# Layer 3 of a four-layer convolution and attention kernel: key tiles two tile rows away scored in packed pieces, and no zero products for the accumulators

## The chip, the core and the metric

The kernel runs on one core of a Trainium2 chip. Its time is the device time of that core in microseconds (us), taken as the median of several executions. A separate execution is recorded by the hardware profiler; all rows of the profile come from that one.

## The reference, cut to what matters

The input is x of shape (4, 256, 48, 48). Three convolution layers come first, each added to its input; the change does not touch them. Layer 3 is a linear attention over windows, again added to its input:

```python
def _L3_conv_ref(x, Wq, Wk, Wv, Wout, bout):      # x: group-normalised
    HEADS, WINDOWS = 8, (1, 2, 4)
    q = sigmoid(einsum('bchw,oc->bohw', x, Wq))   # 8 heads of 32 channels
    k = sigmoid(einsum('bchw,oc->bohw', x, Wk))
    v = einsum('bchw,oc->bohw', x, Wv); v = v / max(norm(v over a head), 1e-12)
    Ik, Ikv = integral(k), integral(k outer v)    # sums over rows and columns
    for w in WINDOWS:                             # box of 48/w by 48/w around each pixel
        wk, wkv = box(Ik, 48 // w), box(Ikv, 48 // w)
        attn = (q . wkv) / (q . wk + 1e-6)
    return Wout @ concat(attn of the three windows) + bout
```

For every query pixel and each of the three windows (48, 24 and 12 pixels wide) the output is the sum of (q . k) v over the keys inside the window, divided by the sum of q . k.

## The kernel before

**Tiles.** The kernel does not build the integral images of k outer v. It multiplies queries with keys block by block. The image is cut into six tile rows of `RB = 8` pixel rows. A query block is one tile row of one batch and of one half of the channels (4 heads), 384 pixels: `order` holds 4 batches x 2 channel halves x 6 tile rows = 48 blocks. The keys of a tile row `a` are three tiles (`c` = 0, 1, 2) of 8 x 16 = 128 keys each. The half windows are `HALVES = [24, 12, 6]`, so the widest window of a query row `rb` reaches keys with |a - rb| up to 3, the middle window up to 2, and the narrow one up to 1.

**Steps.** A step is one tile row of keys and one half of the query columns (`PARTS[half]`), which is two pieces of 320 and 192 columns (280 and 168 at a distance of 3). `scores` writes q . k for 4 heads into two PSUM tiles `s` (two heads each; the pool `ps_s` has two buffers, so a step takes both). Each piece is one product for each head; the four heads sit on four row groups of TensorE and run beside each other. Then follow four *penalty* products (`picks`, `masks`): in those columns that the widest window sees only in part (`strips`), unseen keys get -1024. `masked` takes the scores out of PSUM into a tile `sm`: `widest` is a Relu over the strips on ScalarE, `middle` multiplies by the mask of the middle window on VectorE, and GpSimd multiplies the middle's result by the mask of the narrow window. `sums` then multiplies `sm` by the values `vs` and adds it up in three PSUM accumulators `acc0..2`, one for each window. Columns that the widest window sees whole need no scores: `whole` adds them from a summed state, once a block.

In `masked` the two engines take turns: ScalarE takes the second PSUM tile while VectorE works on the first, then they swap:

```python
if full:
    widest(act, *second); middle(*first)
    widest(act, *first);  middle(*second)
```

A tile row two away (|a - rb| = 2) has two steps like the near ones, but the middle window sees only 3 or 4 of its 8 pixel rows and the narrow one none. A tile row three away is seen by the widest window alone (both `widest`, one on each engine).

**Order.** Every engine runs its instructions in the order of the program (`InOrder`). In `stream` the steps of all blocks follow one another, near and far alternating (`tiles_of`); step n is scored and masked, then step n - 2 (`LAG = 2`) is summed. Between steps `advance` lets other jobs put in work by cost estimates: projections of the next batch (`proj_ps`), key states (`keys_ps`, `kv_ps`), window sums of k on GpSimd (`k_sums`), `norms` (the denominators: DMA loads, differences and products `nhi` on GpSimd, then `norm_ps` on TensorE), `prepare` and `finish` (division and the output product `out_ps`). `turn` and `bank` let a job go on when the step has TensorE time to spare (`time = 1200 + mask_time - sums_time`), `pool_turn` when it has GpSimd time to spare (3600 ns a step less the narrow masks), and `FETCH` holds a job for three steps after a load. `until` makes a step wait, in program order, until a job has been issued: at the start of block i everything for `("done", i - 2)`, in whatever order the jobs then come.

**Accumulators.** `begin` opens a block. `acc1` and `acc2` are first written whole by a product of zeros (`tiled(acc, zeros[:, 0:P], zeros, start=True, stop=False)`), so that every later product can add.

Of the kernel before, what the change touches and what calls it, by code (L numbers as in the profile page):

```python
# [140 lines left out]


# [3 lines left out]
def penalties():  # L146

    got = []
    for half in range(2):
        got.append(((0, half), strips(half), None))  # L150
    for da, (r0, r1) in FAR_ROWS.items():
        for half in range(2):
            got.append(((da, half), PARTS[half], (r0, r1)))
    return got
# [93 lines left out]
def conv_preact_kernel(  # L248
# [1374 lines left out]
    with (  # L1623
# [24 lines left out]
        zeros = wts.tile([P, NB], BF16, name="zeros")  # L1648
        nc.gpsimd.memset(zeros, 0.0)
# [258 lines left out]

        class Block:


            def __init__(self, i, qs):
                self.i, self.qs = i, qs
                self.b, self.ct, self.rb = b, ct, rb = order[i]
                self.tiles = tiles_of(rb)
                self.todo = [
                    [(a, half) for a, half in self.tiles if seen(wi, a, rb)] for wi in range(NW)
                ]
                self.accs = self.stage = None

            def scores(self, a, half):
                r0, r1 = rows_seen(0, a, self.rb)
                ss = [ps_s.tile([P, 2, 512], F32, tag="s", name="s") for _ in range(NPR)]
                at = 0
                for c, x0, x1 in PARTS[half]:
                    n = (x1 - x0) * (r1 - r0)
                    for pr, s in enumerate(ss):
                        for j in range(2):
                            head = slice((2 * pr + j) * D, (2 * pr + j + 1) * D)
                            pe.matmul(  # L1930
                                s[:, j, at : at + n],
                                kvs[self.b, self.ct, a][0][head, c, :],
                                self.qs[head, x0:x1, r0:r1],
                                start=(at == 0),
                                stop=False,
                            )
                    at += n
                lo, hi = strip_columns(half) if rows_whole(a, self.rb) else (0, at)
                first, n = PENALTY_AT[(0 if rows_whole(a, self.rb) else a - self.rb), half]
                for pr, s in enumerate(ss):  # L1940
                    for j in range(2):
                        g = 2 * pr + j
                        rows = slice(g * D, g * D + RB + KC)
                        pe.matmul(
                            s[:, j, lo:hi],
                            picks[rows, :],
                            masks[rows, PEN_AT + first : PEN_AT + first + n],
                            start=False,
                            stop=True,
                        )  # L1950
                return ss

            def parts(self, wi, a, half):

                if wi == 0:
                    return strips(half) if rows_whole(a, self.rb) else PARTS[half]
                return parts_seen(wi, half)

            def masked(self, a, half, ss):

                rb = self.rb
                r0, r1 = rows_seen(0, a, rb)
                wis = [wi for wi in range(NW) if seen(wi, a, rb)]
                full = rows_whole(a, rb)
                offset = {PARTS[half][0][0]: 0}
                offset[PARTS[half][1][0]] = (PARTS[half][0][2] - PARTS[half][0][1]) * (r1 - r0)
                left = {c: x0 for c, x0, _ in PARTS[half]}

                t = smp.tile([P, NPR * SM_ROOM], F32, tag="sm", name="sm")
                at, blocks_, views = 0, [], {}  # L1970
                for wi in wis:
                    y0, y1 = rows_seen(wi, a, rb)
                    ps = self.parts(wi, a, half)
                    for c, p0, p1 in ps:
                        if wi == 0:
                            continue
                        n = HG * (y1 - y0) * (p1 - p0)
                        views[wi, c] = t[:, at : at + n].rearrange(
                            "p (j x r) -> p j x r", j=HG, r=y1 - y0
                        )  # L1980
                        at += n
                    if wi > 0:
                        continue
                    n = sum(p1 - p0 for _, p0, p1 in ps) * (y1 - y0)
                    block = t[:, at : at + HG * n].rearrange("p (j n) -> p j n", j=HG)
                    blocks_ = [block[:, 2 * pr : 2 * pr + 2] for pr in range(NPR)]
                    at, o = at + HG * n, 0
                    for c, p0, p1 in ps:
                        m = (p1 - p0) * (y1 - y0)
                        views[wi, c] = block[:, :, o : o + m].rearrange(  # L1990
                            "p j (x r) -> p j x r", r=y1 - y0
                        )
                        o += m
                assert at <= NPR * SM_ROOM

                def times_mask(engine, wi, c, rows, cols, dst, src):
                    mr = rb * RB + rows[0] - (a * RB - HALVES[wi] + 1)
                    mc = cols[0] - (c * KC - MCOL0[wi])
                    nr, ncol = rows[1] - rows[0], cols[1] - cols[0]
# [5 lines left out]
                many = seen(NW - 1, a, rb)  # L2005

                def middle(s, pr):
                    y0, y1 = rows_seen(1, a, rb)
                    for c, p0, p1 in parts_seen(1, half):
                        at = offset[c] + (p0 - left[c]) * RB  # L2010
                        src = s[:, :, at : at + (p1 - p0) * RB].rearrange(
                            "p j (x r) -> p j x r", r=RB
                        )[:, :, :, y0:y1]
                        dst = views[1, c][:, 2 * pr : 2 * pr + 2]
                        times_mask(dve, 1, c, (y0, y1), (p0, p1), dst, src)

                def widest(engine, s, pr):
                    dst = blocks_[pr]
                    n = dst.shape[2]
                    lo, hi = strip_columns(half) if full else (0, n)  # L2020
                    if engine is act:
                        act.activation(dst, s[:, :, lo:hi], AF.Relu)
                    else:
                        dve.tensor_scalar_max(dst, s[:, :, lo:hi], 0.0)

                first, second = zip(ss, range(NPR))
                if full:
# [7 lines left out]
                if many:  # L2035
                    (y0, y1), (z0, _) = rows_seen(2, a, rb), rows_seen(1, a, rb)
                    seen1 = {c: p0 for c, p0, _ in parts_seen(1, half)}
                    for c, p0, p1 in parts_seen(2, half):
                        src = views[1, c][:, :, p0 - seen1[c] : p1 - seen1[c], y0 - z0 : y1 - z0]
                        times_mask(pool, 2, c, (y0, y1), (p0, p1), views[2, c], src)  # L2040
                return views

            def begin(self):
# [4 lines left out]
                for acc in self.accs[1:]:  # L2048
                    tiled(acc, zeros[:, 0:P], zeros, start=True, stop=False)
# [16 lines left out]
            def sums(self, wi, a, half, sms):  # L2066

                todo, acc = self.todo[wi], self.accs[wi]
                r0, r1 = rows_seen(wi, a, self.rb)
                for k, (c, p0, p1) in enumerate(self.parts(wi, a, half)):  # L2070
                    for j in range(HG):
                        pe.matmul(
                            acc[D * j : D * (j + 1)].rearrange("p (w r) -> p w r", w=W)[
                                :, p0:p1, r0:r1
                            ],
                            kvs[self.b, self.ct, a][1][:, c, j, :],
                            sms[wi, c][:, j],
                            start=(wi == 0 and (a, half) == todo[0] and k == 0),
                            stop=((a, half) == todo[-1] and k == 1),
                        )  # L2080
                if (a, half) == todo[-1]:
# [5 lines left out]

        def seen(wi, a, rb):
# [3 lines left out]
        def tiles_of(rb):  # L2092


            tiles = [
                (a, half)
                for a in sorted(range(NRB), key=lambda a: abs(a - rb))
                for half in range(2)
                if seen(0, a, rb)
            ]  # L2100
            near = [t for t in tiles if seen(NW - 1, t[0], rb)]
            far = [t for t in tiles if t not in near]
            both = min(len(near), len(far))
            return [t for pair in zip(near, far) for t in pair] + near[both:] + far[both:]
# [106 lines left out]
        for a in dict.fromkeys(a for a, _ in tiles_of(0)):  # L2211
# [39 lines left out]
        def done(i):  # L2251
# [11 lines left out]
            (i, a, c, n, n == len(tiles_of(rb)) - 1)  # L2263
            for i, (b, ct, rb) in enumerate(order)
            for n, (a, c) in enumerate(tiles_of(rb))
# [116 lines left out]
```

## Time and profile before

| | us |
|---|---|
| median of 3 executions | 3206.32 (3204.66 to 3215.53) |
| profiled execution, device time | 3220.09 |
| its span, first to last instruction | 3218.3 |
| its first score product (layer 3) | 1412.0 |
| TensorE busy in the span | 2886.4 |
| VectorE, ScalarE, GpSimd busy | 2004.0, 1018.9, 1351.2 |

The profile shows for each engine when it was busy; PE is TensorE's products, PEld its weight loads (they overlap), DVE is VectorE, ACT ScalarE, POOL GpSimd, SP the queue that issues most DMAs. Every instruction of the kernel has one line number, that of the helper which issues it, so that groups are told apart by the names of their tiles: `s<-qs,ks` are scores, `s<-masks` penalties, `sm<-s` and `sm<-s,masks` the masking, `acc<-sm,vs` the sums. One score or sum product of the program appears as two records[...].

### The profile page before, as it was taken

The page shows a single profiled execution, that of the slowest core. Times are in us where ns is not written, and L with a number is a line of the kernel's source. Part 1 is how long each engine was busy: PE and PEld are TensorE (multiplying, and loading weights), DVE is VectorE, ACT ScalarE, POOL GpSimd, SP SyncE. Part 2 cuts the span into 40 slices and gives each one's busy share as a digit, 9 for nine tenths or more (in the row PEclk, how much of TensorE's full clock was granted, in tenths as well). Part 3 has the DMA queues.
Part 4 walks back from the last instruction along what each step waited for, and adds up shares of the span by engine and source line. Part 5 has one row for each costly group of instructions (what it writes and reads, how often), then busy time and mean ns, then how long its engine had stood idle before and what let it go on. Part 6 is the DMA issues. An engine that isn't in the chain of part 4 may idle for free.

```text
span 3218.3 us, 97296 instructions
## 1 busy us (share of the span) xinstructions
PE 2886.4 (90%) x41802; PEld 2014.6 (63%) x41802; DVE 2004.0 (62%) x3907; ACT 1018.9 (32%) x2090; POOL 1351.2 (42%) x1916
## 2 busy tenths in 40 slices
PE   3678999899989978889996999998999999999999
PEld 2456768678776857576663665565566665666665
DVE  7976668647855731466774765676546775455454
ACT  0002211111111153326642335552336533333322
POOL 0000021003001221146788776877846777634443
PEclk9789899999999997989998999999999999999999
DMA  8746513431342253224466555554734455501222
GB/s 273 213 158 196 162 53 116 130 107 60 125 132 92 74 152 114 103 89 140 157 207 173 172 167 164 167 171 152 193 91 145 141 173 162 160 33 54 86 68 67
DMA packets 380033, 433.85 MB, mean 135 GB/s; under 512 B 129844, under 2 KB 335444, under 8 KB 378452
## 3 DMA queue, kind: packets, MB, share of 16 engines
q1 hardware_dynamic: 378403, 425.76, 42.9%
q8 instruction: 331, 5.42, 0.7%
q0 software_dynamic: 144, 1.08, 0.2%
q10 hardware_dynamic: 1056, 0.79, 0.1%
q14 instruction: 99, 0.80, 0.1%
HBM read 287.91 MB, written 140.68 MB: 133 GB/s over the span
## 4 chain that ended last, share of the span: by engine, by line
PE 60%; DVE 12%; POOL 4%; DMA 4%; ACT 4%; issue 3%; SPq 2%; ACTq 0%; DVEq 0%; POOLq 0%
PE s L244 16%; PE cv L244 15%; PE acc L244 14%; PE out_ps L244 5%; PE proj_ps L244 5%; DVE sm L244 3%; PE ap L244 2%; ACT sm L244 2%; SPq L244 2%; DVE l2v L244 2%; POOL nhi L244 1%; POOL sm L244 1%; DVE v L244 1%; PE keys_ps L244 1%; DVE x L244 1%
## 5 line engine op out<-in xcount | busy, mean ns | idle before, releaser
L244 DVE TENSOR_TENSOR sm<-s,masks 128x448 f32<-128x448 f32 (+11 forms) x1536 | 634.6, 470 | 465.5 <-PE s L244 431.5
L244 POOL TENSOR_TENSOR sm<-sm,masks 128x704 f32<-128x704 f32 (+11 forms) x512 | 595.2, 1184 | 559.1 <-DVE sm L244 558.7
L244 ACT ACTIVATE sm<-s 128x384 f32<-128x384 f32 (+2 forms) x864 | 467.5, 545 | 783.1 <-PE s L244 641.0
L244 PE MATMUL s<-qs,ks 32*128 32x320 f32 (+3 forms) x7680 | 601.6, 402 | 46.7 <-ACT sm L244 41.6
L244 PE MATMUL cv<-vx,wt 128*128 128x288 f32 x2080 | 561.6, 426 | 91.1 <-DVE vx L244 49.6
L244 PE MATMUL acc<-sm,vs 128*32 128x128 f32 (+20 forms) x17920 | 607.4, 279 | 1.4 <-issue 1.4
L244 PEld LDWEIGHTS s<-qs,ks 32*128 32x128 f32 x7680 | 376.9, 186 | 278.1 <-issue 111.0
L244 PEld LDWEIGHTS acc<-sm,vs 128*32 128x32 f32 x17920 | 430.2, 110 | 190.5 <-issue 137.6
L244 PEld LDWEIGHTS cv<-vx,wt 128*128 128x128 f32 x2080 | 403.4, 198 | 213.0 <-issue 54.1
L244 POOL MEMSET v<- 128x16 f32 (+1 forms) x120 | 18.7, 216 | 761.1 <-DVE vx L244 634.3
L244 PE MATMUL cv<-v,wl 128*128 128x384 f32 x1152 | 227.9, 358 | 25.1 <-issue 8.0
L244 PEld LDWEIGHTS cv<-v,wl 128*128 128x128 f32 x1152 | 217.7, 198 | 36.6 <-issue 16.4
L244 DVE TENSOR_SCALAR sm<-s 128x896 f32<-128x896 f32 (+1 forms) x96 | 110.9, 1155 | 144.4 <-PE s L244 125.4
L244 PE MATMUL s<-masks 24*128 24x192 bf16 (+2 forms) x1920 | 175.5, 268 | 0.0
L244 POOL TENSOR_TENSOR v<-l2v,v 128x384 fp32r<-128x384 f32 x96 | 108.5, 1160 | 119.3 <-ACT v L244 110.6
L244 PE MATMUL cv<-pad,wl 128*128 128x384 bf16 x864 | 145.5, 331 | 5.1 <-ACT pad L244 5.1
L244 POOL TENSOR_TENSOR nhi<-nhi,nq 128x384 f32<-128x384 f32 x144 | 147.8, 1048 | 0.0
L244 PEld LDWEIGHTS <-wl 128*128 128x128 bf16 x864 | 84.5, 98 | 65.6 <-issue 8.1
L244 PE MATMUL out_ps<-o,wout_sb 128*32 128x384 f32 x1152 | 119.8, 487 | 4.9 <-DVE res L244 2.2
L244 DVE TENSOR_TENSOR pt<-cs 128x184 f32<-128x184 f32 x144 | 119.8, 836 | 0.1
L244 PE MATMUL out_ps<-stage,wout_sb 128*32 128x384 f32 x1152 | 119.4, 486 | 0.0
L244 PE MATMUL ap<-seen,xT 120*128 120x120 f32 (+3 forms) x832 | 118.8, 302 | 0.0
(178 smaller groups left out, 3434.7 us busy)
## 6 DMA issues: line engine op xcount, KB each, us to landing
wt<-wt SPq DMA_DIRECT2D x48, 768.0 KB
kb_d<-pt SPq DMA_DIRECT2D x48, 576.0 KB
rc<-r_d SPq DMA_DIRECT2D x192, 144.0 KB
nhi<-kb_d SPq DMA_DIRECT2D x120, 192.0 KB
nlo<-kb_d SPq DMA_DIRECT2D x88, 192.0 KB
o_d<-stage SPq DMA_DIRECT2D x24, 576.0 KB
o<-o_d SPq DMA_DIRECT2D x24, 576.0 KB
wl<-wl_d SPq DMA_DIRECT2D x16, 768.0 KB
```

What stands on the lines that cost most here:

```text
L244: return lambda *args, **kwargs: self.tc.keep_in_program_order(op(*args, **kwargs))
```

## The change

- The steps are objects (`Step`, `steps_of`) that list their pieces. Near tile rows and those three away keep their two steps each.
- A tile row two away gets one step for both halves that scores only the strips: three pieces of 128 columns (two strips of 64 in one for the middle key tile), 384 columns, and one set of penalties of 384 columns.
- For the middle window of such a tile row only the 3 or 4 pixel rows that it sees are scored, in three pieces (84, 117 and 81 columns for 3 rows; 112, 156 and 108 for 4). They are packed, the largest first, into the strip steps up to 512 columns, and what does not fit goes into a further step that has no strips, no penalties and no Relu. A block with one such tile row has two steps for it as before, a block with two has three in place of four.
- The order within a block becomes: two near steps, then packed or far and near steps alternating, then the rest.
- No zero products: `alike` cuts a sum's piece where some of its columns have been written and some not, and a product to new columns overwrites.
- The penalty table has 384 more columns; `zeros` is not made.

The core of the diff:

```diff
+            def add_strips(self, a):
+                begin = self.columns
+                for c, ranges in STRIPS.items():
+                    at = self.add(a, c, ranges, (0, RB))
+                    self.parts[0].append((a, c, ranges, (0, RB), at, self.columns - at))
+                self.penalties.append((begin, self.columns, PENALTY_AT[0, "strips"][0]))
+                self.lo, self.hi = begin, self.columns
...
+            def add_middle(self, a, c):
+                p0, p1 = cols_seen(1, c)
+                rows = rows_seen(1, a, self.rb)
+                at = self.add(a, c, [(p0, p1)], rows)
+                self.parts[1].append((a, c, [(p0, p1)], rows, at, self.columns - at))
...
+        def steps_of(rb):
...
+                elif abs(a - rb) < FAR:
+                    packed.append(Step(rb))
+                    packed[-1].add_strips(a)
...
+            for n, a, c in sorted(middles, key=lambda m: -m[0]):
+                fits = [st for st in packed if st.columns + n <= 512]
+                if not fits:
+                    packed.append(Step(rb))
+                    packed[-1].lo = packed[-1].hi = 0
+                    fits = packed[-1:]
+                fits[0].add_middle(a, c)
+            far = packed + far
+            got, near = near[:2], near[2:]
+            both = min(len(near), len(far))
+            got += [t for pair in zip(far, near) for t in pair]
+            return got + near[both:] + far[both:]
...
-            def scores(self, a, half):
+            def scores(self, st):
...
-                for c, x0, x1 in PARTS[half]:
-                    n = (x1 - x0) * (r1 - r0)
+                for a, c, ranges, (r0, r1), at, n in st.products:
...
-                                self.qs[head, x0:x1, r0:r1],
+                                of_columns(self.qs[head], ranges, r0, r1),
...
                 first, second = zip(ss, range(NPR))
-                if full:
+                if st.parts[1]:
                     widest(act, *second)
                     middle(*first)
                     widest(act, *first)
...
-                for acc in self.accs[1:]:
-                    tiled(acc, zeros[:, 0:P], zeros, start=True, stop=False)
+                self.reached = [set() for _ in range(NW)]
...
+            def alike(self, wi, ranges, nr):
+                new = [x not in self.reached[wi] for x0, x1 in ranges for x in range(x0, x1)]
+                if all(new) or not any(new):
+                    return [(ranges, 0, len(new) * nr)]
+                ((x0, x1),) = ranges
+                cuts = [0, *(n for n in range(1, len(new)) if new[n] != new[n - 1]), len(new)]
...
-                            start=(wi == 0 and (a, half) == todo[0] and k == 0),
+                                start=not self.reached[wi],
```

## Prediction

> **What bounds the kernel now.** I read the page first, then the chain of waits by stretch, the timeline of TensorE inside a step, the groups by shape, and last the waits where the chain leaves TensorE.
>
> ```profile
> span 3218.3 us, 97296 instructions
> ...
> PE 2886.4 (90%) x41802; PEld 2014.6 (63%) x41802; DVE 2004.0 (62%) x3907; ACT 1018.9 (32%) x2090; POOL 1351.2 (42%) x1916
> ...
> PE 60%; DVE 12%; POOL 4%; DMA 4%; ACT 4%; issue 3%; SPq 2%; ACTq 0%; DVEq 0%; POOLq 0%
> ```
>
> TensorE is busiest and holds most of the chain that ended last. Layer 3 runs from 1412 to 3218 us; the change lies there alone. By batch and channel half (the starts of the blocks lie at 1432, 1657, 1918, 2148, 2388, 2601, 2822 and 3009 us) the chain's TensorE share differs, here for the weakest stretch and the strongest:
>
> ```profile
> by line: PE s L244 18.4%; PE acc L244 16.7%; PE out_ps L244 9.8%; POOL nhi L244 9.4%; SPq L244 7.5%; DMA rc<-r_d 5.6%; POOL sm L244 4.7%; issue 3.6%; DVE sm L244 3.3%; DMA n_d<-ns 2.5%; DMA o<-o_d 2.5%; DMA nhi<-kb_d 2.0%; PE keys_ps L244 1
> ...
> by line: PE acc L244 33.0%; PE s L244 31.6%; PE proj_ps L244 21.4%; PE out_ps L244 3.7%; DMA o<-o_d 2.9%; DVE sm L244 2.9%; SPq L244 2.8%; PE keys_ps L244 1.2%; DVE pt L244 1.1%; ACT sm L244 1.0%; issue 0.6%; DVE ss L244 0.3%; PE kv_ps L244
> ```
>
> The first is batch 1's second half (2148 to 2388): TensorE 46%, and the norms' work (nhi, its DMAs and their issue) much of the rest. The second is batch 2's first half: TensorE 91%. The same view gives 84, 49, 65, 46, 91, 74, 76 and 86% for the eight halves in order.
>
> The rates come from the starts of successive groups on TensorE:
>
> ```profile
> 2399.56 0.83 PE L244 MATMUL out_ps<-stage,wout_sb 128*32 128x384 f32 x8
> 2400.32 1.15 PE L244 MATMUL s<-qs,ks 32*128 32x320 f32 x16
> 2401.29 0.26 PE L244 MATMUL s<-masks 24*128 24x192 bf16 x4
> 2401.48 0.96 PE L244 MATMUL acc<-sm,vs 128*32 128x168 f32 x16
> 2402.26 0.83 PE L244 MATMUL out_ps<-o,wout_sb 128*32 128x384 f32 x8
> 2402.91 0.83 PE L244 MATMUL out_ps<-stage,wout_sb 128*32 128x384 f32 x8
> ...
> 2407.43 0.51 PE L244 MATMUL acc<-zeros 128*32 128x384 bf16 x8
> 2407.75 0.56 PE L244 MATMUL acc<-sm,vs 128*32 128x224 f32 x8
> ```
>
> Four heads' products of 384 columns take 0.65 us (2402.26 to 2402.91), 1.68 ns a column; a step's 512 score columns take 0.97, that is 0.86 at this rate and 0.1 once for the first weight load; 192-column penalties 0.19; a block's zeros 0.32. TensorE is thus paid by columns, and idle time in the chain matters as much as the sums.
>
> ```profile
> 2908.72 0.86 PE L244 MATMUL acc<-sm,vs 128*32 128x112 f32 x32
> 2908.77 0.43 SPq L244 DMA_DIRECT2D vs<-v_d  x1
> 2908.82 1.22 DVE L244 TENSOR_TENSOR sm<-s,masks 128x160 f32<-128x160 f32 x4 [1.40 <-PE s L244]
> 2908.91 1.06 ACT L244 ACTIVATE sm<-s 128x384 f32<-128x384 f32 x2 [1.87 <-PE s L244]
> 2909.51 0.38 POOL L244 TENSOR_TENSOR kv<-state 128x96 f32<-128x96 f32 x1
> 2909.97 0.85 POOL L244 TENSOR_TENSOR kv<-kv,state 128x96 f32<-128x96 f32 x2
> 2910.02 0.97 PEld L244 LDWEIGHTS s<-qs,ks 32*128 32x128 f32 x15 [0.60 <-ACT sm L244]
> ```
>
> This is a step two rows away in batch 3, where little else fills TensorE: scores 1.16, masking 1.2, then TensorE waits for ScalarE before it scores again. Such a step's loop is 2.6 us there, against 3.2 to 3.35 in batches 0 to 2, where filler products hold it.
>
> **The change part by part.** There are 64 pairs of block and tile row two away, half with 3 seen rows and half with 4: 128 steps become 112 (14 for 16 in each half of a batch). TensorE work, by the rates above:
>
> - Score columns: 1024 a pair become 384 + 282 (3 rows) or 384 + 376 (4 rows). Saved 358 and 264 columns, 0.60 and 0.44 us; times 32 each: 33.4 us.
> - Penalties: 128 sets of 192 at 0.19 become 64 of 384. Between 192 (0.19) and the 448-column set (starts 2418.66 to 2418.95 on the same timeline, 0.29) a set of 384 is 0.27. 24.3 - 17.1 = 7.2 us saved.
> - Step heads: 16 fewer steps, each about 0.1 us of exposed load at its head and 0.1 before the sums: 3.4 us.
> - Zeros: 48 x 0.32 = 15.4 us.
> - Sums: the same columns; some pieces are cut to 16 (48 groups) and 32 columns (96 groups).
>
> For those cuts a row stands against a rule. The nearest row:
>
> ```profile
> 2915.41 0.37 PE L244 MATMUL kv_ps<-vs,keys 128*32 128x32 f32 x24
> ```
>
> 24 records in 0.37 us, of which about 0.19 is the tail of the last: some 8 ns from one to the next, 60 ns for eight. The Trainium skill (TensorEngine Tiling (Array Packing), Instruction Overhead) says that each product costs about 60 cycles however few columns it has, which is 25 ns, or 200 ns for eight. By the rule the 144 small groups cost 144 x 0.2 = 29 us, by the row 144 x 0.06 = 8.6; their columns alone are 6.4. I take the row: 2.2 us lost (rule: 22). On the score side no row is near: the trace's smallest score piece has 168 columns, 84-column pieces none. The skill (TensorE: Matmul & The Clock Gate, LDWEIGHTS (loading the stationary operand)) prices a load by its columns over 1.2 GHz, 107 ns for 128 columns, and the 0.1 us at a step's head agrees. A pass over 81 to 117 columns streams for 68 to 98 ns, less than the load. Ends: nothing (loads hidden, as for every piece shown) and, as an estimate from that page, 2 x 107 ns a piece in place of 1.68 a column: 168 ns for each pair with 3 rows and 59 for each with 4, times 32 = 7.3 us. I take the 7.3.
>
> Sum: 33.4 + 7.2 + 3.4 + 15.4 - 2.2 - 7.3 = 50 us of TensorE work, 6.25 in each of the eight halves.
>
> What of it is on the path: the chain's TensorE share. Batches 0 to 2: 6.25 x (0.84 + 0.49 + 0.65 + 0.46 + 0.91 + 0.74) = 25.6 us. In batch 3 the loop of scores and masking counts. ScalarE: 384 elements 492 ns, 896 elements 918 ns, so 768 about 812; VectorE: 120 elements 282 ns, 224 elements 390, 320 elements 485, so 234 about 400 and 312 about 475. A strip step masks in 2 x 0.81 = 1.62 (ScalarE; the turns on a PSUM tile leave VectorE's 0.40 beside it), loop 1.22 + 0.2 + 1.65 = 3.1. The further step has VectorE alone: 1.3, 1.7 or (both rows, four pieces) 3.0 us after 0.5, 0.55 or 0.9 of scores, loops 2.0, 2.45, 4.1. One row away twice: 3.1 + 2.0 or 2.45 against 2 x 2.6; two rows: 6.2 + 4.1 against 10.5. Nothing is gained there. I count 2.5 us for each half of batch 3, from the stretches where output products fill TensorE. Together 30.6 us.
>
> Against it: the four-piece step (16 of them) holds TensorE 4.1 us, while its own scores, a near step's sums (848 columns, 1.42) and one filler of 1.3 make 3.6: up to 0.5 x 16 = 8 us if all bind, less where GpSimd or norms bind anyway. And the waits move, as the next part says. I take 5 us for both. VectorE and ScalarE lose 20 us of work each, off the path. The longer mask table is one GpSimd-queue DMA (1051 KB, landed in 8.6 us at 1146) long before its use: nothing, under 1 us if its cover were gone. SP issues as many DMAs as before. The memset dropped (0.41 us at 1394) is nothing.
>
> Net: 25 us off the profiled execution (3220 to 3195). That one stands 14 us above the median; off the median: 3181.
>
> **The rivals.** *A. All of it pays (3156, 22%).* The fillers flow, the loads hide: the whole 50 us. For: batches 0 to 2 are mostly paid by columns. Against: half shares of 46 and 49%.
>
> *B. Swallowed (3199, 17%).* The late norms set the end of batches 0 and 1, and what TensorE saves before a forced wait is waited there.
>
> ```profile
> 1722.38 3.40 PE L244 MATMUL norm_ps<-nhi,head_sel 128*32 128x384 f32 x6 [15.64 <-POOL nhi L244]
> 1727.99 3.15 PE L244 MATMUL norm_ps<-nhi,head_sel 128*32 128x384 f32 x6 [2.22 <-POOL nhi L244]
> ```
>
> This is such a wait: at a block's start everything open is issued at once and TensorE stands for GpSimd (twelve nhi operations of about 1 us a norm and the loads). That block lasts 65 us where its like lasts 36. The gain is then that of batches 2 and 3 alone (15.3 us) less the four-piece steps in full (8): 7 us.
>
> *C. Slower (3222, 9%).* The plan gives GpSimd 3.6 us a step; 16 steps fewer are 58 us fewer for norms and window sums, whose work is the same. In the fixed instruction order of the two programs, four whole norms sit in one bunch at a block's start before, five after, one of them new in batch 2's second half; the first bunch after the change holds two. A bunch costs 20 (56 against 36 us in batch 1) to 30 us. Against: the outputs of the first block of batch 0's second half leave their bunch and are spread over steps. If two bunches are added and none leaves, 2 x 23 - 31 = +15 us; it decides from the second on.
>
> *D. The change doesn't do what it says (2%).* The instruction order shows the dropped zeros and pieces, so hardly.
>
> **How the numbers follow.** My forecast (25 us off) has 50%: 3181, own range 3166 to 3196. Range over the cases: 3148 (A with a lighter bunch) to 3208 (B whole and the light end of C); about a fifth is left out. A measurement tells about 0.3%, 10 us, from no change: faster is below 3196.7. Forecast, A and a third of B make 0.77; the rest of B and D 0.14; C 0.09.
>
> **What would show it.** Right: score columns down by 8% (19,900 of 242,700), no zeros rows, GpSimd busy the same, steps two rows away at 3.1 and 2 to 4 us in batch 3, first halves of batches 0 to 2 shorter by 4 to 6 us each. Loads: 84-column score pieces spaced by 0.21 us for four heads (hidden: 0.14). Wrong: norm_ps waits on nhi (42.9 us on weight loads now) grown by 20 us or more, or sums of 16 columns spaced by 0.2 us.

## The result and the profile after

| | before | after |
|---|---|---|
| median of 6 executions, us | 3209.27 (3204.66 to 3216.24) | 3193.94 (3186.31 to 3198.54) |
| ratio of after to before, 95% interval | | 0.9948 (0.9928 to 0.9967) |
| profiled execution, us | 3220.09 | 3194.66 |
| layer 3 in the profile, first score product to the last instruction, us | 1806.3 | 1781.1 |

The change makes the kernel faster by 0.5%: 15 us in the medians (11 to 23 by the interval), 25 us between the two profiled executions. The single executions of one kernel differ by up to 37 us in this study (one execution of before is left out: it took 4086 us, with TensorE granted 0.65 of its full clock). Part of it lies ahead of the change: in the profiles layer 3 begins anywhere from 1390 to 1416 us. So beside each ratio I also give the length of layer 3 in the profile. Such a length is that of one execution, and no better than that: the profile of before stands 11 us above the median of its kernel, so of the 25 us between the profiles not all is the change.

The page of the changed kernel, with the lines that answer to those shown of before:

```profile
span 3192.8 us, 98649 instructions
...
PE 2866.5 (90%) x42698; PEld 2024.3 (63%) x42698; DVE 2002.8 (63%) x3779; ACT 994.5 (31%) x1965; POOL 1356.8 (42%) x1915
...
PE 62%; DVE 11%; POOL 4%; DMA 4%; ACT 3%; issue 2%; SPq 2%; ACTq 0%; DVEq 0%; POOLq 0%
...
L251 PE MATMUL s<-qs,ks 32*128 32x320 f32 (+10 forms) x8704 | 589.1, 360 | 34.7 <-ACT sm L251 20.1
L251 PE MATMUL acc<-sm,vs 128*32 128x128 f32 (+19 forms) x18432 | 606.0, 276 | 6.3 <-issue 6.2
...
L251 PE MATMUL s<-masks 24*128 24x192 bf16 (+3 forms) x1664 | 168.3, 284 | 0.0
```

The dropped work shows: score products have more records but 222,800 columns in place of 242,700 (records by columns, over the groups by shape), there is no group with zeros, and GpSimd is as busy as before. The span is 25 us shorter, and TensorE keeps its 90%.

The chain of waits, first for batch 1's second half (2122 to 2350 us), then for batch 2's first (2350 to 2568) and second half (2568 to 2799):

```profile
by line: PE s L251 30.9%; PE acc L251 25.8%; PE out_ps L251 16.5%; DVE sm L251 4.2%; POOL nhi L251 3.6%; ACT sm L251 2.7%; PE norm_ps L251 2.6%; PE proj_ps L251 2.6%; issue 2.3%; PE keys_ps L251 1.9%; DMA nlo<-kb_d 1.7%; PE kv_ps L251 0.6%;
...
by line: PE acc L251 31.7%; PE s L251 28.5%; PE proj_ps L251 18.1%; SPq L251 3.9%; PE out_ps L251 3.6%; DVE sm L251 3.4%; DMA v_d<-vt 2.5%; PE keys_ps L251 1.5%; issue 1.5%; DVE pt L251 1.2%; POOL sm L251 0.9%; DVE cs L251 0.7%; PE kv_ps L2
...
by line: PE s L251 20.0%; PE acc L251 18.7%; PE out_ps L251 13.8%; POOL sm L251 7.4%; POOL nhi L251 6.4%; DMA nq<-qr_d 4.9%; DMA res<-x_d 3.8%; SPq L251 3.8%; PE norm_ps L251 3.4%; issue 3.1%; DVE sm L251 2.1%; DMA rc<-r_d 2.1%; ACT sm L251
```

TensorE's share went from 46 to 81% in the first, from 91 to some 83% in the second, and from 74 to 56% in the third. (These windows, like those of the prediction, begin some 11 us after the halves do. Cut at the halves, 2137, 2377, 2590 and 2811 us before and 2111, 2339, 2557 and 2788 after, the shares are 41, 96 and 68% before and 82, 87 and 51% after.) The share of a stretch is thus no property of the stretch that a change leaves alone: the norms (nhi, their DMAs and what waits for them) left one half and came up in another. By half (from one half's last copy of an accumulator to the next one's), in us:

| batch, half | 0,1 | 0,2 | 1,1 | 1,2 | 2,1 | 2,2 | 3,1 | 3,2 |
|---|---|---|---|---|---|---|---|---|
| before | 232.7 | 252.5 | 238.7 | 235.6 | 218.1 | 211.6 | 196.4 | 206.2 |
| after | 223.8 | 244.6 | 231.0 | 228.3 | 218.0 | 230.7 | 188.6 | 200.1 |

Six halves gain 6 to 9 us each, one nothing, and batch 2's second half loses 19.

That loss is one bunch at the start of a block, TensorE alone:

```profile
2620.26 0.85 PE L251 MATMUL norm_ps<-nhi,head_sel 128*32 128x384 f32 x6
2624.57 3.70 PE L251 MATMUL norm_ps<-nhi,head_sel 128*32 128x384 f32 x6 [3.46 <-POOL nhi L251]
2628.83 0.85 PE L251 MATMUL out_ps<-o,wout_sb 128*32 128x384 f32 x8 [0.56 <-ACT ns L251]
...
2636.90 0.83 PE L251 MATMUL out_ps<-stage,wout_sb 128*32 128x384 f32 x8
2637.54 1.65 PE L251 MATMUL acc<-sm,vs 128*32 128x224 f32 x56
```

Everything that the block must have is issued at once: a norm's products, which wait for GpSimd, and twelve groups of output products one after the other until 2637.54. The step around it lasts 20.6 us, from 2618.5. Two things can be lost: the waiting, some 7.6 us from 2621 on, and the outputs as fillers, which then lack beside the masking of the later steps. The second is argued; no run shows it.

### The profile page after: what moved, and what is told of

It is laid out like the page before. It is cut to its first block, busy times and chain, and to the rows that moved or that the text cites. A ratio compares the mean times of both kernels' runs of the same rounds, so it can differ in the third digit from the quotient of the medians.

```text
span 3192.8 us, 98649 instructions
## 1 busy us (share of the span) xinstructions
PE 2866.5 (90%) x42698; PEld 2024.3 (63%) x42698; DVE 2002.8 (63%) x3779; ACT 994.5 (31%) x1965; POOL 1356.8 (42%) x1915
## 4 chain that ended last, share of the span: by engine, by line
PE 62%; DVE 11%; POOL 4%; DMA 4%; ACT 3%; issue 2%; SPq 2%; ACTq 0%; DVEq 0%; POOLq 0%
PE s L251 16%; PE cv L251 15%; PE acc L251 15%; PE out_ps L251 5%; PE proj_ps L251 5%; PE ap L251 3%; DVE sm L251 2%; DVE l2v L251 2%; SPq L251 2%; POOL sm L251 2%; POOL nhi L251 1%; ACT sm L251 1%; DVE v L251 1%; PE keys_ps L251 1%; DVE x L251 1%
## 5 line engine op out<-in xcount | busy, mean ns | idle before, releaser
L251 DVE TENSOR_TENSOR sm<-s,masks 128x448 f32<-128x448 f32 (+9 forms) x1408 | 619.9, 497 | 437.1 <-PE s L251 379.5
L251 ACT ACTIVATE sm<-s 128x384 f32<-128x384 f32 (+2 forms) x736 | 441.5, 609 | 746.6 <-PE s L251 589.7
L251 PE MATMUL s<-qs,ks 32*128 32x320 f32 (+10 forms) x8704 | 589.1, 360 | 34.7 <-ACT sm L251 20.1
L251 PE MATMUL acc<-sm,vs 128*32 128x128 f32 (+19 forms) x18432 | 606.0, 276 | 6.3 <-issue 6.2
L251 PEld LDWEIGHTS acc<-sm,vs 128*32 128x32 f32 x18432 | 443.0, 110 | 190.2 <-issue 143.4
L251 PEld LDWEIGHTS s<-qs,ks 32*128 32x128 f32 x8704 | 395.1, 186 | 256.2 <-issue 112.0
L251 PE MATMUL s<-masks 24*128 24x192 bf16 (+3 forms) x1664 | 168.3, 284 | 0.0
```

The source lines that it names most:

```text
L251: return lambda *args, **kwargs: self.tc.keep_in_program_order(op(*args, **kwargs))
```

## The experiments

Three explanations stood against each other. *The masking and the columns*: the change brings what its columns bring, and the order of the norms takes part of it back. *Conservation*: waits for norms that are taken out of one block come up in another, so the mending of one bunch brings nothing. *Little by itself*: with the norms gone the change would bring only about 20 us, since TensorE is not what a step two rows away waits for. In the expectations Theory 2 is the first of these, Theory 1 the prediction's reckoning, by the chain's TensorE share and with a plan that hardly matters, and Theory 3 that the masking sets the length of a step. "Profile" below is layer 3 in one profiled execution.

**No zeros, alone and left out.** The first kernel is before without its zero products (`begin` keeps a set of written columns and `sums` cuts at it), the second is after with them:

```diff
 # before, begin()
-for acc in self.accs[1:]:
-    tiled(acc, zeros[:, 0:P], zeros, start=True, stop=False)
+self.reached = [set() for _ in range(NW)]
 # after, begin()
-self.reached = [set() for _ in range(NW)]
+self.reached = [set(), set(range(W)), set(range(W))]
+for acc in self.accs[1:]:
+    tiled(acc, zeros[:, 0:P], zeros, start=True, stop=False)
```

> The kernel before without its zero products (a product to columns not yet written overwrites); pieces, steps and every planner decision as before. Theory 1 (TensorE columns pay by the chain's TensorE share, about 0.7): 15.4 us of products less, 11 us off, ratio to before 0.9965. Rival (a block starts while TensorE waits for the masking anyway): 0 to 3 us, ratio 0.999 to 1.000.

> The changed kernel with the zero products put back; its steps, packing and planner decisions unchanged. The difference to the changed kernel (ratio 0.9948) is the worth of the zeros in the new order. Theory 1: 11 us slower than the changed kernel, ratio to before 0.998. Rival (zeros hidden): as the changed kernel, 0.995.

Measured: 0.9988 (0.9969 to 1.0007), profile 1797.0 (before 1806.3), and 0.9943 (0.9920 to 0.9965), profile 1782.4 (after 1781.1). So by the ratios the zeros are worth some 4 us in the one (9 between the profiles), which the interval doesn't tell from nothing, and nothing in the other. Both are nearer to the rival than to 11 us. In the step that holds them the saving is there (of the steps up to 5.5 us the mean is 3.51 without and 3.70 with them in the first pair, 3.80 and 4.04 in the second), but over a block it is not kept.

**The plan's price of GpSimd.** After with another number for the GpSimd time of a step, and nothing else:

```diff
-pool_time = 3600.0 - far_time(stream[n][1])
+pool_time = 3800.0 - far_time(stream[n][1])   # second kernel: 3724.0
```

> The changed kernel with 3800 ns of GpSimd time planned for a step in place of 3600; the same products. In the fixed order this removes the new bunch of norms in batch 2's second half (and the one in the middle of batch 1's second half). Theory 2 (the change saves about 45 us and bunches that come of fewer steps give 20 to 30 back): batch 2's second half falls from 231 to about 211 us, and the time by 20 us against the changed kernel, ratio to before about 0.988. Theory 1 (the plan hardly matters): ratio as the changed kernel's, 0.995, within 0.003.

> The changed kernel with 3724 ns of GpSimd time planned for a step (the loss of 16 steps in 480 made good). In the fixed order the bunch of batch 2's second half stays, and one appears at the start of batch 1's second half. Theory 2: batch 2's second half stays near 230 us, and the time is that of the changed kernel or 5 to 10 us above, ratio 0.995 to 0.998. If it is the size of the allowance as such and not the bunches that counts: as with 3800, ratio 0.988.

Measured: 0.9969 (0.9954 to 0.9984), profile 1790.6, and 1.0026 (1.0012 to 1.0040), profile 1811.2. With 3800 the bunch in batch 2's second half is gone (218.1 us, from 230.7), and batch 1's second half is better too (216.4, from 228.3). But batch 1's first half went from 231.0 to 246.1, batch 2's first from 218.0 to 225.3. With 3724, 250.5 and 237.8 in batch 1. The same instructions in a slightly different order are 25 us apart (3219.09 against 3193.94), more than the change itself brings. Theory 2 missed both times: the bunch went with 3800, and the 20 us did not come, while with 3724 the kernel is slower than either expectation had it.

**Without the norms' differences and products on GpSimd.** Before and after, both without these two operations:

```diff
-pool.tensor_sub(hi[:, wi, n:RB], hi[:, wi, n:RB], lo[:, wi, n:RB])
-pool.tensor_mul(flat, flat, qf)
```

> The kernel before without the differences and products of the norms on GpSimd (about 240 us of GpSimd work; the denominators are then not those of the reference). Loads, planner and all other instructions as before. Theory 2 (what a bunch at a block's start waits for is the norms' GpSimd work): the excess of steps over 5.5 us, 129 us in the profile of before, falls to about 70 and the time by about 50 us, ratio to before 0.984. Theory 1 (GpSimd is off the path): 0 to 10 us, 0.997 or more.

> The changed kernel without the differences and products of the norms on GpSimd (the denominators are then not those of the reference); planner and all other instructions as in the changed kernel. Theory 2 (the change is worth 45 us where no bunch takes it back): ratio to before 0.970, 45 us below e5. If the change is worth 15 to 25 us wherever it stands: 15 to 25 us below e5, ratio 0.977 to 0.979 if e5 comes to 0.984.

Measured: 0.9901 (0.9871 to 0.9930) and 0.9827 (0.9799 to 0.9854); 22 us between the two medians, 13 in the profiles (1763.6 and 1750.3). Both kernels gain less than Theory 2 had named, and the difference is the 15 to 25 us of the other expectation.

**The norms held back.** After, where a norm of a later block may not put its products on TensorE while a block's start issues what it must have:

```diff
 # norms(), ahead of the products
+while hold and (b, rb) > hold[-1]:
+    yield 1
 # at the start of block i
+hold.append((order[i - 2][0], order[i - 2][2]))
 until(("done", i - 2))
+hold.pop()
```

> The changed kernel; while a block's start forces the outputs of the block two before, the norms of later tile rows are held back and come in the steps after. The same work. In the fixed order three of the five whole norms leave the bunches. Theory 2: batch 0's and batch 2's second halves lose about 15 us each, 20 us or more in all against the changed kernel, ratio to before 0.988. Rival (conservation: norms held back here are waited for in a later bunch, as e3's were): ratio 0.994 to 0.997, with the stalled steps elsewhere.

Measured: 0.9949 (0.9933 to 0.9966), profile 1780.2: as after. The waits of weight loads on nhi, 46.7 us in after, are gone from the list of waits, and no time came of it: batch 1 has 238.2 and 234.2 (from 231.0 and 228.3), batch 0's second half 231.3 (from 244.6), batch 2's second half 224.5. In batch 1 the wait came back under another name, an output product that waits for its factor from the same GpSimd:

```profile
2188.22 1.51 PE L251 MATMUL out_ps<-o,wout_sb 128*32 128x384 f32 x8 [13.65 <-POOL o L251]
2189.50 1.50 PE L251 MATMUL out_ps<-stage,wout_sb 128*32 128x384 f32 x8
```

There the wait is conserved.

**The middle's pieces not packed.** After with a further step of its own for the middle of every tile row two away, as many score columns as after but 480 steps, as before:

```diff
-fits = [st for st in packed if st.columns + n <= 512]
-if not fits:
-    packed.append(Step(rb))
-...
-fits[0].add_middle(a, c)
+if a not in own:
+    own[a] = Step(rb)
+    own[a].lo = own[a].hi = 0
+own[a].add_middle(a, c)
+packed = [t for pair in zip(packed, own.values()) for t in pair]
```

> The changed kernel without sharing: each tile row two away has a strip step of 384 columns and a middle step of its own with three pieces; the same score columns, 480 steps as before the change. Columns alone: 16 step heads more (3.4 us), ratio 0.996. Theory 3 (the masking loop counts: 2.9 us for a strip step and 2.8 for a middle step, 5.7 for a tile row against about 5.2 packed, where masking binds): 10 us slower than the changed kernel, 0.998. Theory 2: with 480 steps the bunch of batch 2's second half is not there, 10 us less: 0.992 to 0.995.

Measured: 1.0050 (1.0032 to 1.0067), profile 1824.6. All the expectations missed: with the columns saved and the zeros gone it is slower than before. Part of it is again a bunch, at the start of batch 3, where nothing had stood before:

```profile
2806.86 3.39 PE L251 MATMUL norm_ps<-nhi,head_sel 128*32 128x384 f32 x6 [3.05 <-POOL nhi L251]
2813.64 3.39 PE L251 MATMUL norm_ps<-nhi,head_sel 128*32 128x384 f32 x6 [3.39 <-POOL nhi L251]
```

The rest of the explanation comes from counting, after the next pairs.

**A block may finish one block later.** Before and after with a third `stage` tile and the demand of a block's start put off by one block; two `kvp` buffers are given up for the room:

```diff
-tc.tile_pool(name="kvp", bufs=2 * NRB, reuse_waits="tile")
+tc.tile_pool(name="kvp", bufs=2 * NRB - 2, reuse_waits="tile")
-self.stage = op.tile([P, NW, NB], F32, tag="stage", name="stage")
+self.stage = op.tile([P, NW, NB], F32, tag="stage", name="stage", bufs=3)
-if i >= 2:
-    until(("done", i - 2))
+if i >= 3:
+    until(("done", i - 3))
```

> The kernel before with three stage tiles in place of two, so that a block's start forces the outputs of the block three before, not two (the key pool gives up two of twelve buffers for the room). The same work. In the fixed order whole norms in bunches fall from four to two. Theory 2 (late norms forced at a block's start cost 10 to 25 us each): ratio to before 0.990 to 0.994. Conservation (what isn't waited for here is waited for later): 0.998 or more.

> The changed kernel with three stage tiles in the same way. Whole norms in bunches fall from five to two, and the one of batch 2's second half is gone. Theory 2: that half falls from 231 to about 208 us, ratio to before about 0.984, and against e9 the change is worth 25 to 35 us. Conservation: ratio 0.993 to 0.996.

Measured: 0.9963 (0.9951 to 0.9975) and 0.9848 (0.9824 to 0.9872; 3160.94 us), profiles 1784.8 and 1756.8. The second is faster than both kernels of this case: 33 us below after. Between the two medians the change is worth 35 us here (3196.31 and 3160.94), 28 in the profiles; the profile of the first stands 19 us below the median of its kernel. The first ratio lies between the two expectations, the second is where Theory 2 had it: here conservation does not hold. The weight loads' waits, first before with the third tile, then after with it:

```profile
PEld s L244 <- ACT sm L244: 94.1, 167, 3.0
...
PEld norm_ps L244 <- POOL nhi L244: 17.5, 19, 3.9
```

```profile
PEld s L251 <- ACT sm L251: 71.2, 118, 2.8
...
PEld norm_ps L251 <- POOL nhi L251: 21.4, 14, 4.9
```

The columns are us in total, times, and the longest. The waits for nhi were 42.9 and 46.7 with two tiles; the wait for the masking is what the change itself lowers. Batch 2's second half is at 206.7 us, batch 2's first at 243.4: one long step remains there (29.7 us at 2290).

**No norms at all.** Before and after with the denominators set to one: no loads, no GpSimd work and no products for them, only the inverse and what follows.

```diff
-loaded = [load(ct) for ct in range(NCT)]
-... (differences, products, norm_ps, ns)
+pool.memset(nr, 1.0)
 start(inverse(b, rb, nr, ...))
```

> The kernel before without the norms: no loads, GpSimd work, products or stores for the denominators; ones are written in their place by the same last step, so that everything after it stands. Takes away what the bunches wait for, in the plan and on the chip. Theory 2: ratio to before 0.975 to 0.98.

> The changed kernel without the norms in the same way. The difference to e11 is the worth of the change where no norm is late. If the change pays by TensorE's columns and only the norms take it back (Theory 2): 40 us below e11, ratio to before 0.963 to 0.967. If its worth is about 20 us by itself, as e5 against e6 has it: 20 us below e11, 0.969 to 0.974.

Measured: 0.9737 (0.9712 to 0.9762) and 0.9665 (0.9641 to 0.9689); 26 us between the medians, 15 in the profiles (1717.2 and 1701.8). The 40 us that the masking and the columns were to bring did not come; the difference is near the theory that gave the change about 20 by itself. (The second ratio by itself lies in the range named for 40 us, since the first kernel, too, came out lower than expected.) By tile row of the block, median block times of these two profiles in us, the very first block left out:

| tile row of the queries | 0 | 1 | 2 | 3 | 4 | 5 |
|---|---|---|---|---|---|---|
| tile rows two away | 1 | 1 | 2 | 2 | 1 | 1 |
| steps, before and after | 8, 8 | 10, 10 | 12, 11 | 12, 11 | 10, 10 | 8, 8 |
| before, no norms | 27.7 | 36.2 | 41.7 | 40.9 | 36.1 | 26.5 |
| after, no norms | 29.0 | 37.3 | 39.5 | 39.7 | 36.3 | 25.5 |

The blocks that lose a step gain 2.2 and 1.2 us, which is less than a step. Blocks with one tile row two away score 264 or 358 columns less; three kinds of them lose 0.2 to 1.3 us, one gains 1.0, and together they gain nothing.

**Counting steps.** From one step's first score product to the next one's, over the profiles (the first steps of layer 3, which follow one another without sums, count as one, and the last step's length is left out):

| | steps | steps over 9.5 us | their excess over 3.4 us each, summed | mean of all others | layer 3 |
|---|---|---|---|---|---|
| before | 478 | 6 | 98 | 3.54 | 1806 |
| after | 462 | 9 | 134 | 3.53 | 1781 |
| after, plan 3800 | 462 | 10 | 145 | 3.52 | 1791 |
| after, plan 3724 | 462 | 11 | 157 | 3.54 | 1811 |
| after, norms held | 462 | 12 | 133 | 3.53 | 1780 |
| after, not packed | 478 | 8 | 128 | 3.51 | 1825 |
| before, third tile | 478 | 6 | 86 | 3.52 | 1785 |
| after, third tile | 462 | 5 | 71 | 3.61 | 1757 |
| before, no norms | 478 | 4 | 43 | 3.47 | 1717 |
| after, no norms | 462 | 7 | 62 | 3.51 | 1702 |

In the mean an ordinary step lasts 3.5 to 3.6 us in all of them: the columns fell by 8% and the mean by 0.4%. What the change takes out is 16 steps, at 3.5 us each 56 us, and the long steps give 36 of it back. The kernel that is not packed has the fewer columns and not the fewer steps: its ordinary steps gain 0.03 x 470 = 13 us, its long ones lose 30, which is about what its layer is longer by. The equal means alone would not show that steps count and not columns, for 50 us of TensorE work less in 16 steps less would leave the mean about where it is, too. The unpacked kernel tells them apart: it has the score columns of after and 16 steps more, for which 3.4 us were expected, and its ordinary steps take 53 us more in all (469 x 3.51 against 452 x 3.53). The planned order differs between the two as well. The kernels with 462 steps stand in the order of their long steps. These are sums over single profiles, and a long step also does work that an ordinary one then has not to do, so the columns don't add up to the layer exactly.

## Why the prediction was right, and where it was wrong

The measured 3194 lies in the range and is faster by more than 0.3%; 15 us by the medians and 25 between the profiles, where 25 was forecast, just above the interval's 11 to 23. That the sum agrees is in good part luck: batches 0 to 2 brought half of what was counted for them, batch 3 nearly three times as much.

**The TensorE work was sized nearly right.** From a step's first score product to the next other product, undisturbed, a near step takes 1.16 us, a strip step with one piece packed in 1.25, a further step of two pieces 0.62 (3 rows) or 0.68 (4), one of four pieces 1.11. One row two away thus saves 2.32 - 1.25 - 0.65 = 0.42 us, two rows save 4.64 - 3.61 = 1.03: 32 x 0.42 + 16 x 1.03 = 30 us, where scores, penalties and loads were put at 33.4 + 7.2 - 7.3 = 33, and 35 with the load at the head of 16 steps. For the new shapes the groups by form give:

```profile
L251 PE MATMUL s<-masks 24*128 24x384 bf16 x256 | 29.7, 325 | 0.0
...
L251 PE MATMUL s<-qs,ks 32*128 32x84 f32 x256 | 16.6, 280 | 0.2
...
L251 PE MATMUL acc<-sm,vs 128*32 128x16 f32 x384 | 11.1, 181 | 0.0
```

The means are those of single records with their tails; the spacing is read from the starts. Penalties of 384 columns are 272 ns apart for four heads (0.27 was taken). Sums of 16 columns are 60 ns apart for eight records where another sum follows, as in the row of before and not as by the rule of the Trainium skill (TensorEngine Tiling (Array Packing), Instruction Overhead), 60 cycles for each product, estimated at 0.2 us for eight: the 22 us of that rule did not come. The score pieces behave as if bound by their loads, as the Trainium skill (TensorE: Matmul & The Clock Gate, LDWEIGHTS (loading the stationary operand)) let one expect: pieces of 84 and of 108 columns both take 204 ns for four heads with two records each, 102 ns a record (page: 107), where their columns alone would take 141 and 181. Over all pieces that is 7.9 us; 7.3 was taken.

**The zeros were mis-sized.** 15.4 us of work, of which about 8 was counted on the path of batches 0 to 2 by the chain's share; by the ratios nothing to 4 came, and neither is clear of nothing.

**The step that failed is the chain's TensorE share as the part of the saving that pays in batches 0 to 2.** It says who was last in the old order. It gave 25.6 us for batches 0 to 2; the halves of the profile give 8.9 + 7.9 + 7.7 + 7.3 + 0.1 - 19.1 = 12.8. The first halves were to gain 4 to 6 us each; they gained 8.9, 7.7 and, in batch 2, with TensorE at 91%, nothing at all (218.1 and 218.0). The work was saved where it did not bind: blocks with one row two away have as many steps as before, and of such a block's steps the strip step lasts 3.74 us and the further one 2.79 in batches 0 to 2 without norms (medians), with near steps of 3.63 and 3.55 behind them: 13.7 for the four. Before, the two steps two rows away last 3.34 and 2.81 and the near steps behind them 3.90 and 3.55: 13.6. What I had argued for batch 3 alone, that a single row two away gains nothing, holds in the other batches too.

**Batch 3 was mis-sized the other way.** 2.5 us a half were taken, 7.8 and 6.1 came. The masking was costed right: in the groups by form

```profile
L251 ACT ACTIVATE sm<-s 128x768 f32<-128x768 f32 x128 | 97.4, 809 | 74.8 <-PE s L251 70.9 <-POOL sm L251 2.0 <-DVE sm L251 1.8
L251 DVE TENSOR_TENSOR sm<-s,masks 128x312 f32<-128x312 f32 x64 | 30.4, 475 | 22.7 <-PE s L251 20.3 <-POOL sm L251 2.1
...
L251 DVE TENSOR_TENSOR sm<-s,masks 128x234 f32<-128x234 f32 x64 | 25.2, 397 | 41.2 <-ACT sm L251 19.5 <-PE s L251 17.4 <-POOL sm L251 4.1
```

809, 475 and 397 ns stand against 812, 475 and 400. The loop is there too, in the timeline of TensorE, VectorE and ScalarE for a strip step, up to the scores of the next:

```profile
2850.51 1.48 PE L251 MATMUL s<-qs,ks 32*128 32x128 f32 x29
...
2852.27 0.40 DVE L251 TENSOR_TENSOR sm<-s,masks 128x234 f32<-128x234 f32 x1 [1.42 <-PE s L251]
2852.43 1.51 ACT L251 ACTIVATE sm<-s 128x768 f32<-128x768 f32 x2 [0.83 <-PE s L251]
2853.27 0.40 DVE L251 TENSOR_TENSOR sm<-s,masks 128x234 f32<-128x234 f32 x1 [0.60 <-ACT sm L251]
2853.84 1.28 PE L251 MATMUL s<-qs,ks 32*128 32x320 f32 x16
```

From 2850.51 to 2853.84 the strip step takes 3.33 us, ScalarE's two Relus in the middle of it; ten of the sixteen strip steps of batch 3 take 3.32 or 3.33 (3.1 taken). Further steps of two pieces measured 1.8 to 3.0 (2.0 and 2.45 taken), those of four pieces 3.8 in the first half and 5.9 in the second, where output products stand in them (4.1). The 2.6 us of an old step two rows away were read in one place; the 32 such steps of batch 3 have a median of 2.93. The gain of the first half comes from elsewhere: its first block went from 36.7 to 29.0 us, and the longest step in it (11.3 us at 2802, the block's start, with output products) to 6.8. The 6.1 us of the second half are spread over its six blocks, 0.2 to 2.0 us each, and I can't place them.

**The waits moved as rival C said, but once.** Against the four-piece steps and the bunch together 5 us were taken. The new bunch in batch 2's second half alone cost 19 (13 by the run with 3800). The waits of norm products on nhi went from 42.9 to 46.7 us, not up by 20, and batches 0 and 1 did not lose a second one: rival C's condition, two bunches added and none gone, was not met. The run with 3724 comes close to it: long steps of 32.2 us (at 1878) and 20.2 us (at 2644) stand where before has one of 12.6 and none, and it is 9 us slower than before, where C had put 15.

**What stays open.** Why the mean ordinary step stays at 3.5 us, in the near steps too, is shown only for the strip steps of batch 3 (the masking loop); in batches 0 to 2 fillers, norms and masking lie together, and no run took the masking away. The change also puts the steps of a block in another order, and no run has the old steps in the new order. It may count: without norms the near steps, whose columns are the same, went from 3.89 to 3.54 us and those three rows away from 2.90 to 3.36 (means of the steps up to 9.5 us), so what a step takes depends on what stands around it. How much of the third tile's gain is the deadline and how much the tile was not separated.

## What to carry to other kernels

Before columns are saved, ask whether a step is paid by columns or by its turn: here 8% fewer score columns in as many steps brought little (13 us in the ordinary steps of the unpacked kernel, the zeros' share among them), and without norms it was mainly the blocks with a step less that gained, 1 to 2 us each. A share of the chain is not a rate of exchange; take out a saving by the piece of work that it shortens, block kind by block kind, and look whether the loop around it becomes shorter. In a program whose order comes from a planner, every change also draws a new order; here one constant of the plan moved the time by up to 25 us, more than the change itself. So judge the change by a pair with the planned work taken out, and then relax the deadline that makes the bunches, which brought 12 us before the change and 33 after it.

## What the runs showed of the hardware

**A long row need not be slow work.** The six records of norm products at 2624.57 take 3.70 us where those at 2620.26 take 0.85. The timeline joins like instructions into one row, with the waits between them; the rows of GpSimd and of the weight loads show three waits:

```profile
2623.04 3.69 POOL L251 TENSOR_TENSOR nhi<-nhi,nq 128x384 f32<-128x384 f32 x3
2624.56 0.14 PEld L251 LDWEIGHTS norm_ps<-nhi,head_sel 128*32 128x32 f32 x2 [4.15 <-POOL nhi L251]
2625.62 0.18 PEld L251 LDWEIGHTS norm_ps<-nhi,head_sel 128*32 128x32 f32 x2 [0.92 <-POOL nhi L251]
2626.78 0.18 PEld L251 LDWEIGHTS norm_ps<-nhi,head_sel 128*32 128x32 f32 x2 [0.98 <-POOL nhi L251]
```

Each of the three products waits for its own operation of GpSimd, three of which take 3.69 us.

**The granted clock falls when TensorE has stood.** The granted clock is the share of its full clock that TensorE is given. In the same bunch it is 1.00 from 2618 to 2624.5, 0.57 from 2624.5 to 2628.5 and 1.00 again from 2628.5, where the output products start. In the run with the norms held, the low clock reaches into the work behind the wait of 13.65 us: from 2188.2 to 2191.2 the clock is 0.50, the groups of output products at 2188.22, 2189.50 and 2190.78 start 1.28 us apart, and those from 2193.98 on, at a clock of 1.00, 0.65 us. That adds some 1.6 us to the wait.

**Type and time of a product.** In before each of the 3840 fp32 score products leaves two records and each of the 1920 bf16 penalties one. A set of four fp32 output products of 384 columns takes 0.65 us from start to start, and two sets of four bf16 zero products of the same shape 0.32 together: a quarter of the time for a set.
